# Another fixed order for the prologue of a decoder layer: weight casts ahead of the second half's norm halves, keys evicted first

## The chip, the cores and the metric

The kernel runs on one core of one Trainium2 chip. The metric is the time of one execution on the device in microseconds (us), lower is better; the kernel is run three times and the median stands for it. One of the executions was recorded by the hardware profiler, and all rows shown below are from that one.

A core has five engines with an instruction queue each: PE (TensorE, matrix products; PEld is its weight load), DVE (VectorE), ACT (ScalarE), POOL (GpSimd) and SP (SyncE, which here issues all DMA transfers). [...]

## The reference, cut to what matters

A decoder layer on x of 8 sequences x 128 tokens x 512 features, float32:

```python
x = x + attn(layernorm(x), w_q, w_k, w_v, w_o)   # 32 query heads, 8 key heads, head size 128, causal
x = x + xattn(ctx, ctx, layernorm(x))            # softmax over keys of ctx, no weights
x = x + ffn(layernorm(x), gate, up, down)        # 4-bit weights with scales and zeros, silu(gate)*up
```

Only the start of the first line is touched here: the norm of x, the products with w_q (512 x 4096), w_k and w_v (512 x 1024 each), and the first attention steps. The first line's heart is

```python
q = (h @ w_q).reshape(B, S, 8, 4, 128); k = (h @ w_k).reshape(B, S, 8, 128); v = ...
scores = einsum("bqhgd,bkhd->bhgqk", q, k) * 128 ** -0.5
probs = softmax(where(causal, scores, -inf)); attn = einsum("bhgqk,bkhd->bqhgd", probs, v)
return attn.reshape(B, S, 4096) @ w_o
```

## The kernel before, in words

**Two halves per number.** Products are made of 16-bit pieces: each operand is held as a high float16 part and a low one (the rest), and a product takes three matmuls (`mm3`, L161 to L163: high x high, high x low, low x high). So nearly each tile is made in two steps: ACT casts the high part (`split`, L115), then DVE or POOL subtracts it from the source for the low part (L118). For weights that are cast "direct", ACT scales and casts (`convert`, L349) and DVE makes the low part (L350).

**Weight scales.** A weight tile is scaled by a power of two that is found from its squares: `sumsq` (L259, ACT, squares with a running sum), then `scales_parts`: a copy on DVE (L282), a tiny matmul with ones that adds over partitions (L286 or L289, into ps_n), and three small DVE steps (L295, L303, L311). `next(...)` on such a generator emits its next part.

**Norm.** A tile of x (128 tokens, xr0 to xr7) gets its mean and variance on DVE (`ln_stats`, L400 to L406), then POOL raises the variance to -1/2 (rstd, L412) and writes the normed tile h (L414) in `ln_apply`. The tiles are handled in two halves of four. The first half's h is transposed on TensorE (`h_pe`, L392, then split by ACT and DVE into hT). The second half's h takes another way (`h_dma`): ACT casts the high half hb (L115), POOL makes the low half (L118), and SP issues a DMA transpose into hT (L431).

**Groups and tiles.** The work goes by groups of one key head and its four query heads (8 groups, 2 halves). `proj_k` makes a group's keys for a half (512 tokens), `proj_q` one of its four query heads, `proj_v` the values for one tile of 128 tokens and a pair of groups. Their results land in a PSUM bank each (ps_k, ps_q, ps_v, all of one ring of two banks) and are evicted by ACT and DVE in the generators' second part: keys to k2 (L115, L118), queries to qh and ql, values to v (L494, L495), followed by two DMA copies vd of the value's first rows (L501). `att_s` is an attention step's first part: score matmuls (ps_sc), mask and row maximum (DVE, L558), exponential (ACT, L515), scaling by the sums (POOL, L525 and L572), the split into pb (ACT cast L115, POOL low part L118), and a DMA transpose of pb to pt (L586); pb has two buffers, pt three. `att_v` multiplies pt with the values (ps_at, L595 and on), `att_o` with w_o (ps_o), added to xr (L612).

**What sets the order.** The program is built by a tile scheduler that orders instructions by its own estimate of time. The prologue is kept out of that: everything that `begin()` emits is chained inside `in_order()`, which ties each instruction to the one before it on the same engine. So the order of the calls in `begin()` is the order on each engine, with one exception: instructions whose names are in `loose` are free, and these are those of `att_s(0, 0)`. After `begin()` the scheduler decides, so a change in `begin()` also moves later instructions about; which of them stay where they are can be seen only in the built program. The store zd (L734) puts the unpacked 4-bit zeros, made by DVE (L721) from zw (L715), into memory, from where they are read back spread over the partitions (zi, L750); srow (L637) are the scales of the same weights.

All DMA transfers are issued by SP from one queue. The first 13 (x, and the weights of the first group) are issued at once.

Of the kernel before, what the change touches and what calls it, by code (L numbers as in the profile page):

```python
# [23 lines left out]
GH = 4  # L24
NH = 32
HB = 4
# [27 lines left out]
def tile_decoder(  # L54
# [19 lines left out]
    nc = tc.nc  # L74
# [56 lines left out]
    loose = set()  # L131
# [109 lines left out]
    def sumsq(kind, g, i, j, n=1):  # L241

        raw = raw_t[kind, g]
        if kind == "q":
            view = raw[:, :, j * P : (j + 1) * P]
        elif kind == "c":
            view = raw.unsqueeze(1)
        elif kind in "kv":
            view = raw
        else:  # L250
            view = raw[:, i * GH // n : (i + 1) * GH // n, :]
        key = "ss", kind, g
        if key not in raw_t:
            cols = GH if kind == "q" else n
            raw_t[key] = small.tile([P, cols], F32, name="ss" + kind, tag="ss" + kind)
        col = j if kind == "q" else i
        junk = work.tile([P, 2 * TH], BF16, name="junk", tag="junk", bufs=1)
        free = view.shape[1] * view.shape[2]
        ins = nc.scalar.activation(  # L259
            junk[:, :free].rearrange("p (a t) -> p a t", a=view.shape[1]),  # L260
            view,
            AF.Square,
            accum_out=raw_t[key][:, col : col + 1],
        )
        if pace:
            issue_after(ins, pace["exp"])
        return ins
# [5 lines left out]
    def scales_parts(kind, g, cols=None):  # L273

        ss = raw_t["ss", kind, g]
        n = ss.shape[1]
        c0, c1 = cols or (0, n)
        m = c1 - c0  # L280
        sb = small.tile([P, m], BF16, name="sb", tag=f"sb{m}")
        nc.vector.tensor_copy(sb, ss[:, c0:c1])  # L282
        ps = bank("a", [P, GH], "ps_n")
        w = m if kind == "q" else 1
        if w == m:
            nc.tensor.matmul(ps[:, :w], ones, sb, start=True, stop=True)  # L286
        else:
            for i in range(m):
                nc.tensor.matmul(  # L289
                    ps[:, :1], ones, sb[:, i : i + 1], start=i == 0, stop=i == m - 1  # L290
                )
        yield
        norm = ONORM if kind == "o" else WNORM
        r = small.tile([P, w], F32, name="r", tag=f"r{w}")
        nc.vector.tensor_scalar(  # L295
            r.bitcast(I32),
            ps[:, :w].bitcast(I32),
            0x7F000000,
            1,
            ALU.bitwise_and,  # L300
            ALU.logical_shift_right,
        )
        nc.vector.tensor_scalar(r, r, ROOT, 2.0**64 / norm, ALU.max, ALU.mult)  # L303
        if kind == "c":
            sc_t[kind, g] = scx[:, g : g + 1]
        if (kind, g) not in sc_t:
            sc_t[kind, g] = small.tile(
                [P, GH if kind == "q" else 1], F32, name="sc" + kind, tag="sc" + kind
            )
        sc = sc_t[kind, g]  # L310
        nc.vector.reciprocal(sc[:, c0:c1] if kind == "q" else sc, r)  # L311
        yield
# [50 lines left out]
    def prep_wq(g, j, direct=False):  # L363
        hi = wqp.tile([P, KT, P], F16, name="wqh", tag="wqh")
        lo = wqp.tile([P, KT, P], F16, name="wql", tag="wql")
        wq_t[g * GH + j] = hi, lo
        raw = raw_t["q", g][:, :, j * P : (j + 1) * P]
        return convert(hi, lo, raw, sc_t["q", g][:, j : j + 1], direct)
# [28 lines left out]
    def ln_stats(b):  # L397
        st = small.tile([P, 6], F32, name="st", tag="st")
        mv = small.tile([P, 2], F32, name="mv", tag="mv")
        nc.vector.bn_stats(st, xr[b])  # L400
        nc.vector.bn_aggr(mv, st)
        rs = small.tile([P, 2], F32, name="rs2", tag="rs2")
        nc.vector.tensor_scalar(
            rs[:, 0:1], mv[:, 1:2], EPS, ASCALE**-2, ALU.add, ALU.mult
        )
        nc.vector.tensor_scalar(rs[:, 1:2], mv[:, 0:1], -1.0, None, ALU.mult)  # L406
        ln_t["rs", b] = rs

    def ln_apply(b):
        rs = ln_t.pop(("rs", b))  # L410
        rstd = small.tile([P, 1], F32, name="rstd", tag="rstd")
        nc.gpsimd.tensor_tensor(rstd, rs[:, 0:1], mhalf, ALU.pow)  # L412
        h = deqp.tile([P, H], F32, name="h", tag=("qr", "zi")[b % 2], bufs=2)
        nc.gpsimd.tensor_scalar(h, xr[b], rs[:, 1:2], rstd, ALU.add, ALU.mult)  # L414
        ln_t["h", b] = h
# [30 lines left out]
    def proj_q(g, half, j, pieces=(slice(0, TH),)):  # L446

        ps = bank("j", [P, TH], "ps_q")
        if j % 2 == 0:
            q_t[g, half, j // 2] = [  # L450
                qp.tile([P, HB, 2, 2, HQ], F16, name="q" + p, tag="q" + p) for p in "hl"
            ]
        hi, lo = q_t[g, half, j // 2]
        for cs in pieces:
            proj(ps[:, cs], wq_t[g * GH + j], half, cs)
            yield
            bs = slice(cs.start // P, cs.stop // P)
            split(
                hi[:, bs, :, j % 2, :],
                lo[:, bs, :, j % 2, :],  # L460
                ps[:, cs].rearrange("p (b a t) -> p b a t", a=2, t=HQ),
            )
            yield
# [300 lines left out]
    for m in "gud":  # L764
        _, _, _, ngr, n = quant[m]
# [9 lines left out]
    def begin():  # L775

        warm = const.tile([P, TH], BF16, name="warm")
        nc.vector.memset(warm, 0.0)
        psw = bank("s", [P, TH], "ps_w")

        def fill(n):
            for _ in range(n):
                nc.tensor.matmul(psw, warm[:, :P], warm, start=True, stop=True)

        fill(11)
        load_x(0)
        fetch_wk(0)
        for b in range(1, HB):
            load_x(b)
        fetch_wq(0)  # L790
        fetch_wv(0)
        for b in range(HB, B):
            load_x(b)
        fetch_wo(0)
        fetch_wk(1)

        kgen = proj_k(0, 0, ((0, 2), (2, 4)))
        h = {b: h_pe(b) for b in range(HB)}
        q = [proj_q(0, 0, j) for j in range(GH)]
        ln_stats(0)  # L800
        sumsq("k", 0, 0, 0)
        ln_apply(0)
        sk = scales_parts("k", 0)
        next(sk)
        ln_stats(1)
        next(sk)
        ln_apply(1)
        next(h[0])
        fill(6)
        ln_stats(2)  # L810
        ln_apply(2)
        next(h[0])
        next(h[1])
        fill(5)
        ln_stats(3)
        ln_apply(3)
        prep_wk(0, True)
        next(h[1])
        next(h[2])
        sumsq("q", 0, 0, 0)  # L820
        sq = scales_parts("q", 0, (0, 1))
        next(sq)
        fill(2)
        next(h[2])
        next(sq)
        next(h[3])
        prep_wq(0, 0, True)
        next(kgen)
        next(h[3])
        for j in range(1, GH):  # L830
            sumsq("q", 0, 0, j)
        next(kgen)
        sq, sv, so = scales_parts("q", 0, (1, GH)), scales_parts("v", 0), scales_parts("o", 0)
        next(sq)
        ln_stats(4)
        ln_apply(4)

        next(q[0])
        next(sq)
        prep_wq(0, 1, True)  # L840
        next(kgen)
        sumsq("v", 0, 0, 0)
        next(sv)
        h_dma(4)
        ln_stats(5)
        ln_apply(5)
        next(q[0])
        next(sv)
        next(q[1])
        prep_wq(0, 2, True)  # L850
        h_dma(5)
        ln_stats(6)
        ln_apply(6)
        prep_wq(0, 3, True)
        next(q[1])
        next(q[2])
        h_dma(6)
        ln_stats(7)
        ln_apply(7)
        prep_wv(0, 0, True)  # L860
        soft_scale(0)
        next(q[2])
        next(q[3])
        last_h = h_dma(7)
        fetch_wq(1)
        prep_wv(0, 1, True)
        v = [proj_v(0, b) for b in range(HB)]
        next(q[3])
        next(v[0])
        n = len(nc.cur_bb.bb.instructions)  # L870
        att_s(0, 0)
        loose.update(i.name for i in nc.cur_bb.bb.instructions[n:])
        next(v[1])
        next(v[0])
        next(v[2])
        next(v[1])
        next(v[3])
        next(v[2])
        next(v[3])
        for i in range(2):  # L880
            sumsq("o", 0, i, 0, 2)
        for _ in so:
            pass
        out_scale(0)
        prep_wo(0, 0, True)
        prep_wo(0, 1, True)
        return last_h

    with in_order():
        last_h = begin()  # L890
# [467 lines left out]
```

## Time and profile before

| | us |
|---|---|
| median of 3 runs | 669.97 (669.09 to 671.97) |
| the profiled execution | 669.99 |
| its span, first to last instruction | 668.2 |
| TensorE busy | 632.3 (95%) |
| DVE, ACT, POOL busy | 478.1, 443.3, 389.4 |
| TensorE idle from 12.6 to 35 us | 5.69 |
| TensorE idle from 35 to 55 us | 3.72 |
| TensorE idle from 55 to 90 us | 0.05 |

Times within the profile count from the start of the span. A row of the timeline gives start and duration, engine, line, operation, what is written and read with the shapes, how many are merged, and in brackets the idle time of the engine before it with the instruction that ended it. TensorE ran at its full clock (granted share 0.999), and its weight loads overlap its matmuls.

### The profile page before, as it was taken

Reading aid. Unit: us, or ns where it says so; the run is one execution under the profiler, and the core shown is the slowest. Engines: PE = TensorE matmul, PEld = TensorE weight load, DVE = VectorE, ACT = ScalarE, POOL = GpSimd, SP = SyncE. Lnnn points to the kernel's source line nnn. Section 1 sums busy time; section 2 is a strip of 40 time slices with the busy share of each in tenths; the row PEclk is TensorE's granted clock in tenths of the full one; section 3 lists DMA queues with packets and bytes.
Section 4 is the critical chain, followed back from the end, with each engine's and each line's share of the span. In section 5 each row is a group of like instructions: output and inputs, shape, how many; then the busy total and the mean of one; then the engine's idle time right before and its main releaser. Section 6 shows DMA issues by size and latency. Waiting matters only on the chain.

```text
span 668.2 us, 12402 instructions
## 1 busy us (share of the span) xinstructions
PE 632.3 (95%) x3978; PEld 339.1 (51%) x3978; DVE 478.1 (72%) x1492; ACT 443.3 (66%) x1239; POOL 389.4 (58%) x576
## 2 busy tenths in 40 slices
PE   7798999999999999999999999999998989899996
PEld 4365545455555556555555555445544434444442
DVE  6756687765757776675778465677676779889896
ACT  4587486655757575656678566875566478977774
POOL 5668297744747795556588587753577247422520
PEclk9999999999999999999999999999999999999999
DMA  9266344854454665455445624143543252102002
GB/s 311 51 161 172 100 62 122 170 119 149 111 153 96 180 134 153 102 153 141 146 117 150 147 36 119 46 102 72 87 60 69 39 85 51 34 18 63 2 1 63
DMA packets 117757, 69.34 MB, mean 104 GB/s; under 512 B 84174, under 2 KB 100577, under 8 KB 117692
## 3 DMA queue, kind: packets, MB, share of 16 engines
q1 hardware_dynamic: 117692, 68.55, 43.1%
q8 instruction: 31, 0.51, 0.3%
q14 instruction: 34, 0.28, 0.1%
HBM read 42.12 MB, written 2.20 MB: 66 GB/s over the span
## 4 chain that ended last, share of the span: by engine, by line
PE 49%; POOL 18%; issue 9%; DMA 8%; DVE 8%; ACT 7%; SPq 0%; POOLq 0%; DVEq 0%; ACTq 0%
PE ps_c L1093 6%; PE ps_c L1094 6%; PE ps_o L163 5%; PE ps_o L161 5%; PE ps_o L162 5%; DMA pt<-pb 4%; PE ps_q L161 4%; PE ps_q L163 4%; PE ps_q L162 4%; POOL pb L118 4%; POOL s L572 3%; DMA rawq<-in_L_attn_w_q_dram 2%; POOL wql L118 2%; POOL wol L118 2%; POOL rawo L355 2%
## 5 line engine op out<-in xcount | busy, mean ns | idle before, releaser
L515 ACT ACTIVATE s<-s,negm 128x64 f32<-128x64 f32 (+1 forms) x256 | 93.2, 367 | 35.6 <-DVE negm L558 35.4
L161 PE MATMUL ps_o<-woh,ah 128*128 128x512 f16 x256 | 97.1, 379 | 2.4 <-ACT ah L115 2.2
L161 PE MATMUL ps_q<-hT,wqh 128*128 128x512 f16 x256 | 97.0, 379 | 1.9 <-DVE ql L118 1.0
L163 PE MATMUL ps_o<-woh,al 128*128 128x512 f16 x256 | 97.1, 379 | 1.5 <-DVE al L118 1.4
L162 PE MATMUL ps_o<-wol,ah 128*128 128x512 f16 x256 | 97.0, 379 | 0.0
L163 PE MATMUL ps_q<-hT,wql 128*128 128x512 f16 x256 | 97.0, 379 | 0.0
L162 PE MATMUL ps_q<-hT,wqh 128*128 128x512 f16 x256 | 97.0, 379 | 0.0
L612 DVE SCALAR_TENSOR_TENSOR xr<-ps_o,unsc,xr 128x512 f32<-128x512 f32 x64 | 47.9, 748 | 43.4 <-PE ps_o L163 40.6
L118 POOL TENSOR_TENSOR pb<-s,pb 128x256 f16<-128x256 f32 (+1 forms) x128 | 71.9, 577 | 11.1 <-ACT pb L115 8.4
L558 DVE CUSTOM_DVE_ANT_0 s<-ps_sc,mask,soft 128x64 f32<-128x64 f32 (+1 forms) x256 | 67.2, 311 | 6.5 <-PE ps_sc L163 4.7
L525 POOL TENSOR_SCALAR rec<-rec 128x4 f32<-128x4 f32 x64 | 14.9, 233 | 93.8 <-DVE rec L523 91.9
L572 POOL TENSOR_TENSOR s<-s,rec 128x128 f32<-128x128 f32 (+1 forms) x128 | 63.9, 520 | 4.5
L118 DVE TENSOR_TENSOR ql<-ps_q,qh 128x512 f16<-128x512 f32 x64 | 44.0, 687 | 29.3 <-ACT qh L115 29.1
L115 ACT CAST pb<-s 128x128 f16<-128x128 f32 (+1 forms) x128 | 43.3, 351 | 30.7 <-POOL s L572 29.3
L115 ACT CAST ah<-ps_at 128x512 f16<-128x512 f32 x64 | 37.2, 582 | 19.1 <-PE ps_n L289 7.1
L355 POOL TENSOR_TENSOR rawo<-rawo,sco 128x512 f32<-128x512 f32 x30 | 31.5, 1056 | 29.9 <-DVE sco L311 29.9
L515 ACT ACTIVATION_READ_ACCUMULATOR s<-s,negm 128x1 f32 x256 | 48.5, 190 | 0.0
L118 DVE TENSOR_TENSOR al<-ps_at,ah 128x512 f16<-128x512 f32 x64 | 43.8, 684 | 4.7 <-ACT ah L115 4.2
L115 ACT CAST qh<-ps_q 128x512 f16<-128x512 f32 x64 | 36.8, 575 | 15.3 <-PE ps_q L163 15.2
L1102 ACT ACTIVATE ps_c<-ps_c,rTu 128x512 f32<-128x512 f32 (+1 forms) x57 | 36.7, 662 | 14.7 <-PE ps_c L1094 14.4
L1104 DVE TENSOR_SCALAR ps_c<-ps_c,rTg 128x512 f32<-128x512 f32 (+1 forms) x56 | 40.5, 750 | 7.2 <-PE ps_c L1094 7.1
L161 PE MATMUL ps_sc<-k,qh 128*128 128x128 f16 (+1 forms) x256 | 41.2, 206 | 2.7 <-ACT qh L115 2.6
(225 smaller groups left out, 1737.7 us busy)
## 6 DMA issues: line engine op xcount, KB each, us to landing
rawq<-in_L_attn_w_q_dram SPq DMA_DIRECT2D x8, 1024.0 KB, 7.0
rawo<-in_L_attn_w_o_dram SPq DMA_DIRECT2D x8, 1024.0 KB, 6.0
zi<-zd SPq DMA_DIRECT2D x26, 256.0 KB, 3.6
vd<-v SPq DMA_DIRECT2D x64, 64.0 KB, 2.3
qr<-_L_ffn_down_qweight_dram SPq DMA_DIRECT2D x10, 256.0 KB, 3.5
xr<-in_x_dram SPq DMA_DIRECT2D x8, 256.0 KB, 5.2
rawk<-in_L_attn_w_k_dram SPq DMA_DIRECT2D x8, 256.0 KB, 3.4
rawv<-in_L_attn_w_v_dram SPq DMA_DIRECT2D x4, 512.0 KB, 7.6
```

The costliest lines, as they stand in the source:

```text
L115: a = nc.scalar.copy(hi, src)
L118: b = (lo_eng or nc.vector).tensor_tensor(lo, src, hi, ALU.subtract)
L161: nc.tensor.matmul(ps, lh, rh, start=start and i == 0, stop=False)
L162: nc.tensor.matmul(ps, lh, rl, start=False, stop=False)
L163: nc.tensor.matmul(ps, ll, rh, start=False, stop=stop and i == n - 1)
L355: a = nc.gpsimd.tensor_tensor(raw, raw, wide.to_broadcast(list(raw.shape)), ALU.mult)
L515: exp = nc.scalar.activation(v, v, AF.Exp, bias=negm[:, j : j + 1], scale=-1.0, accum_out=sums[:, j : j + 1],)
L558: nc.vector.tensor_tensor_reduce(view, flat(ps, cols[j]), masks[j // 2], soft_t[g][:, j % 2 : j % 2 + 1], BIG, ALU.add, ALU.min, negm,)
L572: mul = nc.gpsimd.tensor_tensor(v, v, rec[:, 2 * k : 2 * k + 2].unsqueeze(2).to_broadcast([P, 2, (k + 1) * HQ]), ALU.mult,)
L612: return nc.vector.scalar_tensor_tensor(xr[b], ps, unsc_t[g], xr[b], ALU.mult, ALU.add)
L1093: nc.tensor.matmul(ps, lh, rh, start=r == 0, stop=False, skip_group_check=r > 0)
L1104: nc.vector.tensor_scalar(ps, ps, sc, None, ALU.mult)
```

## The change

`begin()` is written in another order; no call is added or taken away. In the new order

- the statistics and the norm of tile 3 (`ln_stats(3)`, `ln_apply(3)`) come ahead of the second part of the transposes of tiles 0 and 1, and those of tile 4 ahead of the cast of the first query weight;
- the squares of the query weights are no longer taken three in a row: that of query 1 comes ahead of tile 4's statistics, those of 2 and 3 behind both halves of the key product, and the eviction of the keys (the third `next(kgen)`) comes ahead of `h_dma(4)` and the second query weight's cast;
- the query weights 1, 2 and 3 are cast (`prep_wq`) ahead of `h_dma(5)`, and both value weights (`prep_wv`) ahead of `h_dma(6)` and `h_dma(7)`; the squares and the scale of the value weight come behind the second and third query weight's cast;
- `h_dma(6)` and `h_dma(7)` stand behind most of the query evictions;
- the matmuls of `att_s(0, 0)` are no longer free: only its instructions on other engines are in `loose`;
- the generators of v and of w_o's scales are made at another place, which emits nothing.

```diff
@@ -797,6 +797,7 @@
         kgen = proj_k(0, 0, ((0, 2), (2, 4)))
         h = {b: h_pe(b) for b in range(HB)}
         q = [proj_q(0, 0, j) for j in range(GH)]
+        v = [proj_v(0, b) for b in range(HB)]
         ln_stats(0)
         sumsq("k", 0, 0, 0)
         ln_apply(0)
@@ -809,67 +810,69 @@
         fill(6)
         ln_stats(2)
         ln_apply(2)
+        ln_stats(3)
+        ln_apply(3)
         next(h[0])
         next(h[1])
         fill(5)
-        ln_stats(3)
-        ln_apply(3)
+        next(h[1])
         prep_wk(0, True)
-        next(h[1])
         next(h[2])
         sumsq("q", 0, 0, 0)
-        sq = scales_parts("q", 0, (0, 1))
-        next(sq)
+        sq0 = scales_parts("q", 0, (0, 1))
+        next(sq0)
+        next(h[2])
+        next(h[3])
         fill(2)
-        next(h[2])
-        next(sq)
+        next(sq0)
         next(h[3])
+        sumsq("q", 0, 0, 1)
+        ln_stats(4)
+        ln_apply(4)
         prep_wq(0, 0, True)
         next(kgen)
-        next(h[3])
-        for j in range(1, GH):
-            sumsq("q", 0, 0, j)
         next(kgen)
-        sq, sv, so = scales_parts("q", 0, (1, GH)), scales_parts("v", 0), scales_parts("o", 0)
+        sumsq("q", 0, 0, 2)
+        sumsq("q", 0, 0, 3)
+        sq = scales_parts("q", 0, (1, GH))
         next(sq)
-        ln_stats(4)
-        ln_apply(4)
-
         next(q[0])
         next(sq)
+        next(kgen)
+        h_dma(4)
         prep_wq(0, 1, True)
-        next(kgen)
-        sumsq("v", 0, 0, 0)
-        next(sv)
-        h_dma(4)
         ln_stats(5)
         ln_apply(5)
+        prep_wq(0, 2, True)
+        sumsq("v", 0, 0, 0)
         next(q[0])
+        next(q[1])
+        prep_wq(0, 3, True)
+        sv = scales_parts("v", 0)
+        next(sv)
+        h_dma(5)
         next(sv)
         next(q[1])
-        prep_wq(0, 2, True)
-        h_dma(5)
+        next(q[2])
         ln_stats(6)
         ln_apply(6)
-        prep_wq(0, 3, True)
-        next(q[1])
+        prep_wv(0, 0, True)
+        prep_wv(0, 1, True)
         next(q[2])
-        h_dma(6)
         ln_stats(7)
         ln_apply(7)
-        prep_wv(0, 0, True)
         soft_scale(0)
-        next(q[2])
+        h_dma(6)
+        next(q[3])
         next(q[3])
         last_h = h_dma(7)
         fetch_wq(1)
-        prep_wv(0, 1, True)
-        v = [proj_v(0, b) for b in range(HB)]
-        next(q[3])
         next(v[0])
         n = len(nc.cur_bb.bb.instructions)
         att_s(0, 0)
-        loose.update(i.name for i in nc.cur_bb.bb.instructions[n:])
+        loose.update(
+            i.name for i in nc.cur_bb.bb.instructions[n:] if i.engine != mybir.EngineType.PE
+        )
         next(v[1])
         next(v[0])
         next(v[2])
@@ -877,6 +880,7 @@
         next(v[3])
         next(v[2])
         next(v[3])
+        so = scales_parts("o", 0)
         for i in range(2):
             sumsq("o", 0, i, 0, 2)
         for _ in so:
```

## The prediction

> **What bounds the kernel now.** I read the page first, then busy time by stretches, then each engine's timeline through the prologue.
>
> ```profile
> PE 632.3 (95%) x3978; PEld 339.1 (51%) x3978; DVE 478.1 (72%) x1492; ACT 443.3 (66%) x1239; POOL 389.4 (58%) x576
> 12.60:35.00 22.40, 16.71 (x108) 9.12 (x107) 14.90 (x41) 12.65 (x25) 11.23 (x12) 1.00 0.43 113
> 35.00:55.00 20.00, 16.28 (x136) 10.90 (x135) 11.44 (x54) 18.01 (x66) 13.12 (x24) 1.00 0.73 188
> 55.00:90.00 35.00, 34.95 (x225) 19.15 (x223) 23.59 (x87) 21.22 (x60) 19.81 (x26) 1.00 0.42 100
> ```
>
> The stretches give length, then busy time of PE, PE's weight loads, DVE, ACT, POOL. TensorE is full from 55 us (34.95 of 35). Before that it idles 22.40 - 16.71 = 5.69 us and 20.00 - 16.28 = 3.72 us. The matmuls are the same in both kernels, so whatever the new order takes out of these 9.41 us should move the rest forward. TensorE's timeline shows where the idle time lies (start, duration, then in brackets the idle time and its releaser):
>
> ```profile
> 20.35 0.16 PE L286 MATMUL ps_n<-sb,ones 128*128 128x1 bf16 x1 [1.30 <-DVE sb L282]
> 26.87 0.38 PE L161 MATMUL ps_q<-hT,wqh 128*128 128x512 f16 x1 [1.01 <-DVE ql L118]
> 31.16 0.27 PE L161 MATMUL ps_v<-wvh,hT 128*128 128x256 f16 x1 [1.48 <-DVE ql L118]
> 33.73 0.27 PE L162 MATMUL ps_v<-wvl,hT 128*128 128x256 f16 x1 [0.40 <-DVE wvl L350]
> 46.26 0.39 PE L161 MATMUL ps_q<-hT,wqh 128*128 128x512 f16 x1 [0.86 <-DVE r L303]
> 52.76 0.20 PE L161 MATMUL ps_sc<-k,qh 128*128 128x64 f16 x1 [2.43 <-ACT qh L115]
> ```
>
> A matmul's row lasts 0.38 us, though the next one starts 0.22 us later, so each printed gap is about 0.16 us below the matmul time lost. With that, and with gaps of 0.81, 0.23, 0.75 and 0.37 us at 14.85, 16.27, 32.56 and 33.04, I count 7.0 us lost up to 35 us and, with 0.59 at 53.48, 4.3 us from there to 55 us.
>
> Why the evictions and weights are late is seen on ACT and POOL:
>
> ```profile
> 23.80 0.62 ACT L115 CAST hb<-h 128x512 f16<-128x512 f32 x1 [2.08 <-POOL h L414]
> 24.33 0.72 ACT L349 ACTIVATE wqh<-rawq,scq 128x512 f16<-128x512 f32 x1
> 24.51 1.16 POOL L118 TENSOR_TENSOR hb<-h,hb 128x512 f16<-128x512 f32 x1 [0.74 <-ACT hb L115]
> 25.62 1.01 POOL L412 TENSOR_TENSOR rstd<-rs,mhalf 128x1 f32<-128x1 f32 x1
> 26.73 0.77 POOL L414 TENSOR_SCALAR h<-xr,rs,rstd 128x512 f32<-128x512 f32 x1
> 27.54 0.62 ACT L115 CAST hb<-h 128x512 f16<-128x512 f32 x1 [2.02 <-POOL h L414]
> 31.27 0.62 ACT L115 CAST hb<-h 128x512 f16<-128x512 f32 x1 [2.02 <-POOL h L414]
> ```
>
> This is a ring with one turn in 3.73 us (27.54 - 23.80; 31.27 - 27.54). ACT waits 2.0 us for POOL's h, three times. Behind that wait, in ACT's order, stand a weight cast and a query eviction that don't need h: wqh for query 3 at 24.33, wvh at 28.06 and 31.80. So the norm of the second half's tiles, wanted only at 40 us, paces the first half's weights, wanted at once.
>
> [...] the weight's scale was ready at 17.8 us and its cast waited until 24.33. [...] the cast's low half (L350) takes 0.75 us at 18.62 but 1.13 us at 25.08, under POOL's 1.16 us at 24.51; then rstd (L412) takes 1.01 us at 25.62 instead of 0.55. [...] vd at 36.31 us, behind the 1 MB rawq of 34.48, took 4.3 us to land, where the vd issued from 43 to 46 us took 2.0.
>
> **The change, part by part.** No instruction is added or removed. I laid the new order end to end, each instruction at the later of its engine being free and its inputs being there, with durations from these rows. All new times below are such estimates. The first 13 loads stay in place.
>
> *Keys evicted and statistics taken earlier.* Statistics of tile 4 (0.68, 0.18 and two of 0.15 us) stand ahead of the first query weight and start at 13.8 instead of 16.1; rstd follows at 15.0 (17.4 before) and h ends at 16.8 (18.8). The key eviction comes before the second query weight's cast and runs at 15.7 (18.5). Cost: the squares of query weights 2 and 3 end later against the small norm matmul, which waits 0.71 us (0.23 before). That is the price of this part, 0.5 us.
>
> *Weight casts ahead of the norm halves.* The scale of weights 1 to 3 is there at 16.9. ACT casts at 17.4, 18.0 and 20.2 (before 17.87, 21.00, 24.33; 0.62 us apart). [...] The V scale comes later, since its squares (1.06 us) stand behind two casts: its copy runs on DVE at 22.8 and its small matmul at 23.0, with TensorE waiting 1.40 us (as before, 1.47). V casts: 23.7 and 24.4 (before 28.06, 31.80); low halves done at 27.0 (33.7).
>
> TensorE then: query 0 16.2 to 18.7, query 1 to 21.6 (0.27 us wait for its low weight), query 2 23.0 to 25.6, query 3 to 28.1, first V to 29.4, then 0.58 us for query 3's low half, and no gap until the first half's last V at 35.8. That was at 40.02. Lost time: 0.71 + 0.27 + 1.40 + 0.58 = 3.0 against 7.0: **4.0 us**.
>
> *Score matmuls held in order.* The first scores no longer slip between query matmuls. They are 12 matmuls of under 0.06 us spacing; moving them costs nothing but the 0.58 us counted, which stalls the next V with them.
>
> *Norm halves behind.* POOL: rstd of tile 5 at 20.4, tile 6 at 25.4, tile 7 at 28.7; the last two low halves (1.16 us each) end at 31.2 and 32.3. Their transposes wait on SP one behind the other (1.24 us to issue), are issued at 31.2 and 32.5, and land 3.1 us later, the last at 35.6 (before: 33.15 and some 36.2). The second half's keys need all four, and TensorE comes there at 35.8. What was 3.8 us of slack is 0.2: this edit is free only just.
>
> *SP queue.* The next rawq goes out at 33.8 instead of 34.48, still behind the four transposes. The zeros and scale loads (zw, srow) now follow the first two attention transposes pt. Before, SP sat in `38.26 3.11 SPq L501` until rawq had landed and issued the first pt at 43.19; pb has two buffers, so ACT's third pb cast waited for that landing (46.04), the fourth until 48.65, and the query eviction behind them came at 52.13: the 2.43 us gap. New: pt at 37.5, landing at 41.6 behind rawq, and the next at about 44; the casts run at 41.6 and 45.1. The gap becomes 1.27 us; those beside it stay (1.2 and 0.6). Saved: **1.2 us**.
>
> Sum: 4.0 + 1.2 = 5.2, of which I take 5.1. From the second half's keys on, the large order on TensorE is the same but for interleavings, and what it waits for there moves along. The profiled run took 669.99 us, 1.8 outside its span of 668.2; the median of the runs is 669.97. Span 663.1, time **664.9 us**.
>
> **Rivals.**
>
> *Given back in part.* The norm of tiles 5 to 7 becomes the bound: slack is 0.2 us, and the weights' low halves now stand close together on DVE, each able to hold POOL 0.46 us (1.01 - 0.55). Two or three more collisions, or transposes 1.24 us apart landing slower than the lone ones seen, put the last landing at 36.8 to 38: TensorE waits 1 to 2.2 us, gain 2.9 to 4.1, time 666 to 667. For it: the thin slack. Against: I have two such holds in the sum already. Chance 0.18.
>
> *More than counted.* Waits of attention for pt after 90 us (0.71 us at 93.81 printed, three others) belong to an interleaving that changes; if they go, 2 to 3 us more, about 662. Nothing in the profile asks for it. Chance 0.07.
>
> *Slower.* The pt ahead of 93.81 stands behind the store zd:
>
> ```profile
> 86.90 0.26 SPq L734 DMA_DIRECT2D zd<-z  x1
> 87.36 2.05 SPq L586 DMA_TRANSPOSE pt<-pb  x1
> 92.96 0.83 SPq L750 DMA_DIRECT2D zi<-zd  x2
> ```
>
> zi waits for zd's landing, so zd takes 6.06 us and holds that pt with it, and TensorE already waits there. zd hangs on zw, which is loaded 7.4 us later now (42.5 for 35.07). Each us by which zd comes after 81.8 (86.90 - 5.1) is lost in full; at 86.9 the gain is gone, and past 90.3 the kernel is slower by over 0.5%; at 91 it takes 674 us. Against: zw lands by 46 and DVE first reads it after 60. Chance 0.04.
>
> That the change does nothing is excluded: the orders differ on all engines.
>
> **How the numbers follow.** 0.5%, 3.35 us, is about what a measurement of this kernel tells from no change. The likeliest case has 0.71, with 663 to 666.5 as its own range. Faster by over 0.5% (below 666.6): 0.71, 0.07 and a third of the 0.18, less a little for the edge of the likeliest: 0.82. Within 0.5%: 0.14. Slower: 0.04. The range, 662.3 to 667.8, leaves out the slower case and the ends of the others.
>
> **What would show it.** Right: ACT's 2.0 us waits before hb (L115) gone as a series, wvh casts near 24, second-half keys on TensorE near 36, idle up to 55 us down from 9.4 to about 4.9 as printed. Wrong: a TensorE wait of over 1 us before the second half's ps_k released by hT's transpose (first rival); a longer wait at ps_at behind zd (third); wql or rstd rows above 1 us in most rounds.

## The result, and the profile after

The changed kernel takes 667.36 us (median of 8 runs, 665.86 to 668.79) against 670.06 us of the kernel before: a ratio of 0.9955, 95% interval 0.9937 to 0.9972. In a second comparison, with runs of the kernel before on the same chip beside it, it took 666.58 us (5 runs, 666.11 to 668.30) against 670.88: 0.9944, interval 0.9930 to 0.9957. It is faster, by 2.7 and 4.3 us where 5.1 were predicted; 667.4 lies within the range of 662.3 to 667.8 and above the likeliest case's own range of 663 to 666.5.

The first profiled execution took 668.19 us (span 666.4), the one of the second comparison 666.48 (span 664.7). I call the two profiles the first and the second one after. The same three stretches as before, columns as there (length; busy time of PE, PE's weight loads, DVE, ACT, POOL; then granted clock, DMA share, GB/s), in the first profile after:

```profile
12.60:35.00 22.40, 20.34 (x155) 12.82 (x155) 18.27 (x66) 15.31 (x41) 12.26 (x14) 1.00 0.47 113
35.00:55.00 20.00, 16.08 (x102) 8.72 (x100) 10.10 (x36) 15.90 (x53) 14.73 (x25) 0.92 0.89 198
55.00:90.00 35.00, 35.00 (x224) 19.24 (x223) 23.21 (x93) 22.09 (x66) 20.03 (x28) 1.00 0.47 100
```

and the second of them in the second profile:

```profile
35.00:55.00 20.00, 15.99 (x103) 8.87 (x101) 9.91 (x36) 15.83 (x52) 14.98 (x25) 1.00 0.90 204
```

Up to 35 us TensorE's idle time fell from 5.69 to 2.06 us. From there to 55 us it rose, from 3.72 to 3.92 and 4.01 us. The gain of the first stretch is kept; the second stretch, where 1.2 us were promised, gave nothing. (The granted clock of 0.92 in the first profile is taken up at the end.)

TensorE's timeline of the first profile after says where (start, duration, and in brackets the idle time and its releaser):

```profile
23.36 0.16 PE L286 MATMUL ps_n<-sb,ones 128*128 128x1 bf16 x1 [0.79 <-DVE sb L282]
31.09 0.20 PE L163 MATMUL ps_sc<-k,ql 128*128 128x64 f16 x1 [0.54 <-DVE ql L118]
...
36.93 0.39 PE L161 MATMUL ps_k<-hT,wkh 128*128 128x512 f16 x1
...
46.80 0.28 PE L161 MATMUL ps_v<-wvh,hT 128*128 128x256 f16 x1 [0.87 <-DVE ql L118]
50.04 0.20 PE L161 MATMUL ps_sc<-k,qh 128*128 128x64 f16 x1 [1.75 <-ACT qh L115]
```

Counted as in the prediction (start of a matmul, minus the start of the one before, minus that one's own pace), the waits from 12.6 to 35 us were 7.0 us before and are 2.9 us now: 0.60 at 16.79, 0.41 at 20.24, 0.95 at 23.36, 0.23 at 28.79, and 0.70 at 31.09. The second half's keys start at 36.93 us, and at 36.59 in the second profile, against 40.02. After that, the wait of 1.00 us at 43.17 stayed as it was, that before the scores fell only from 2.59 to 1.92 us (50.04), and one of 1.03 us at 46.80 is new.

ACT and SP show why. First SP, then ACT, of the first profile after (start, time on the engine; for SP the time to issue):

```profile
35.18 0.54 SPq L219 DMA_DIRECT2D rawq<-in_L_attn_w_q_dram  x1
35.81 3.08 SPq L501 DMA_DIRECT2D vd<-v  x5
38.99 1.34 SPq L586 DMA_TRANSPOSE pt<-pb  x1
```

```profile
44.32 0.61 ACT L115 CAST pb<-s 128x256 f16<-128x256 f32 x2 [1.94 <-DMA pt<-pb]
...
46.55 1.32 ACT L349 ACTIVATE woh<-rawo,sco 128x512 f16<-128x512 f32 x2
47.78 0.59 ACT L115 CAST pb<-s 128x256 f16<-128x256 f32 x2
...
49.41 0.58 ACT L115 CAST qh<-ps_q 128x512 f16<-128x512 f32 x1
```

The first pt goes out at 38.99 and lands at 44.25 (by its semaphore in the trace). Until then ACT waits 1.94 us in front of its third pb cast. The square of rawq that stands behind that cast starts only at 44.83, though rawq had landed at 41.32: here ACT took nothing out of turn. From 44.32 to 49.41, for 5.09 us, it works without a pause through two pairs of pb casts, three squares, a query eviction and three woh casts, and only then makes the qh for which TensorE stands still.

### The profile page after: what moved, and what is told of

It reads as the page before. It is cut to its first block, busy times and chain, and to the rows that moved or that the text cites. A ratio compares the mean times of both kernels' runs of the same rounds, so it can differ in the third digit from the quotient of the medians.

```text
span 666.4 us, 12404 instructions
## 1 busy us (share of the span) xinstructions
PE 633.2 (95%) x3978; PEld 339.7 (51%) x3978; DVE 474.1 (71%) x1492; ACT 444.4 (67%) x1239; POOL 389.3 (58%) x576
## 4 chain that ended last, share of the span: by engine, by line
PE 49%; POOL 19%; issue 10%; DVE 8%; DMA 7%; ACT 6%; SPq 0%; POOLq 0%; DVEq 0%; ACTq 0%
PE ps_c L1097 6%; PE ps_c L1098 6%; PE ps_o L163 5%; PE ps_o L161 4%; PE ps_o L162 4%; POOL pb L118 4%; PE ps_q L161 4%; PE ps_q L163 4%; PE ps_q L162 4%; DMA pt<-pb 4%; POOL s L572 4%; POOL wql L118 2%; POOL wol L118 2%; POOL rawo L355 2%; POOL rawq L355 2%
## 5 line engine op out<-in xcount | busy, mean ns | idle before, releaser
L115 ACT CAST pb<-s 128x256 f16<-128x256 f32 (+1 forms) x128 | 43.4, 352 | 30.4 <-POOL s L572 27.8
L163 PE MATMUL ps_sc<-k,ql 128*128 128x128 f16 (+1 forms) x256 | 42.7, 206 | 1.1 <-DVE ql L118 1.0
```

The source lines that it names most:

```text
L115: a = nc.scalar.copy(hi, src)
L163: nc.tensor.matmul(ps, ll, rh, start=False, stop=stop and i == n - 1)
```

## The experiments

Two theories stood after this. A: rawq, the 1 MB load that is issued ahead of pt, holds pt back, and with it pb and qh. D, which came up after the first four runs: what stands ahead of qh in ACT's own order holds it back, whenever pt lands. They do not exclude each other: qh comes after both. Waits are given as counted above, and each ratio is to runs of the kernel before beside it on the same chip (medians of 670.85 us for e1 to e4, 670.88 for e7 to e9, 670.60 for e10 and e11).

| kernel | median us | ratio to before, 95% interval |
|---|---|---|
| change, first / second comparison | 667.36 / 666.58 | 0.9955 [0.9937, 0.9972] / 0.9944 [0.9930, 0.9957] |
| e1, change with rawq early | 667.65 | 0.9951 [0.9934, 0.9968] |
| e2, change with the scores loose | 668.86 | 0.9963 [0.9947, 0.9979] |
| e3, first part alone | 670.42 | 0.9992 [0.9982, 1.0001] |
| e4, second part alone | 669.47 | 0.9981 [0.9971, 0.9991] |
| e7, change with woh behind qh | 664.70 | 0.9908 [0.9894, 0.9921] |
| e8, as e7, rawq early | 663.67 | 0.9892 [0.9878, 0.9905] |
| e9, as e8, two squares behind qh too | 660.99 | 0.9851 [0.9838, 0.9864] |
| e10, as e9, rawq back | 662.70 | 0.9881 [0.9859, 0.9903] |
| e11, before, woh and squares behind qh | 666.62 | 0.9942 [0.9925, 0.9960] |

### The two parts alone (e3, e4)

e3 is the kernel before with the change's lines up to the key eviction; from there it is as before:

```diff
         ln_apply(2)
+        ln_stats(3)
+        ln_apply(3)
         next(h[0])
...
+        sumsq("q", 0, 0, 1)
+        ln_stats(4)
+        ln_apply(4)
         prep_wq(0, 0, True)
...
         next(sq)
+        next(kgen)
         prep_wq(0, 1, True)
-        next(kgen)
         sumsq("v", 0, 0, 0)
         next(sv)
```

> The kernel before with the first part of the change alone: keys evicted first, statistics of tiles 3 and 4 sooner, squares of the query weights spread; the weight casts stay behind the norm halves as before. If the gain comes from the casts' place (the prediction), ACT's waits of about 2.0 us before hb stay, and the time is within 0.7 us of the kernel before (669.3 to 670.7). If the early statistics carry the gain, 667 to 668.

e4 is the reverse: the old order up to the first query projection, the change's order from the key eviction on.

> The kernel before with the second part of the change alone: weight casts ahead of the norm halves of tiles 5 to 7, scores' matmuls in order, the scale loads behind the attention transposes; keys and early statistics as before. If the casts' place carries the gain, ACT's waits of 2.0 us before hb go and the time is 2 to 3 us below the kernel before (667 to 668), about the changed kernel's. If the early statistics are needed for it, it stays within 1 us of the kernel before, with TensorE waiting for the first query weights near 20 us or for tile 4 to 7's transposes near 36 us.

e3 measured 670.42 us against 670.85, with the interval just reaching 1: little or nothing, as expected from it. In its profile ACT waits in the old ring:

```profile
23.23 0.62 ACT L115 CAST hb<-h 128x512 f16<-128x512 f32 x1 [2.08 <-POOL h L414]
23.75 0.72 ACT L349 ACTIVATE wqh<-rawq,scq 128x512 f16<-128x512 f32 x1
```

e4 measured 669.47 us, 1.4 below before, between the two outcomes that I had named (2 to 3, or less than 1). The second half's keys start at 38.35 us, so it gets about half of the 3.1 to 3.4 us by which the change moves them. What it lacks shows on TensorE:

```profile
20.46 0.39 PE L161 MATMUL ps_q<-hT,wqh 128*128 128x512 f16 x1 [1.07 <-ACT wqh L349]
```

and on ACT, where an hb cast waits ahead of those weights:

```profile
19.16 0.62 ACT L115 CAST hb<-h 128x512 f16<-128x512 f32 x1 [1.99 <-POOL h L414]
19.69 1.33 ACT L349 ACTIVATE wqh<-rawq,scq 128x512 f16<-128x512 f32 x2
```

In the changed kernel that hb cast, of tile 4, waits 0.77 us and starts at 17.77, since tile 4's statistics were taken earlier. So the parts seem not to be additive: alone they give 0.4 and 1.4 us, together 2.7 to 4.3. With such differences the times alone leave this likely, not sure; TensorE's waits are the better sign. The prediction treated the first part as a price of 0.5 us for the second. It is rather what lets the casts start: without it TensorE waits 1.24 us at 20.46 and 0.72 us at 21.62 for the query weights, against 0.41 us with it.

### The scores loose again (e2)

```diff
-        loose.update(
-            i.name for i in nc.cur_bb.bb.instructions[n:] if i.engine != mybir.EngineType.PE
-        )
+        loose.update(i.name for i in nc.cur_bb.bb.instructions[n:])
```

> The changed kernel with one part undone: the matmuls of the first scores may slip between those of the query and V projections again, as in the kernel before. By the prediction this part costs nothing but moves a wait of 0.5 us: time within 0.5 us of the changed kernel. Rival: held in order, the scores make the following V matmuls wait for query 3's low half (0.70 us of lost time at 31.09), and loose they give 0.5 to 0.7 us back.

668.86 us, with runs from 666.16 to 670.06: unclear against the changed kernel. The first score matmuls do move ahead of query 3, but the wait for ql stays (0.88 us at 30.84, 0.70 in the change), so the rival, that holding them costs 0.5 to 0.7 us, finds no support: the wait was not given back. The second half's keys then wait 0.84 us for the last hT transpose (37.37). The scheduler also ordered many later instructions differently here, so I read no more into the time.

### rawq out of pt's way (e1), and the measure (a2)

```diff
         h_dma(5)
+        fetch_wq(1)
         next(sv)
...
         last_h = h_dma(7)
-        fetch_wq(1)
         next(v[0])
```

> The changed kernel with one edit: the 1 MB load of the next query weights (rawq) is issued right behind the transpose of tile 5's norm halves instead of behind that of tile 7, so some 9 us earlier on SP. Theory A (the second term of the prediction failed because the first attention transpose pt stood behind rawq): the first pt lands by 42 us instead of 44.25, ACT's wait of 1.94 us before its third pb cast shrinks below 0.5, TensorE's new gap of 1.03 us at 46.80 goes and the one of 1.92 at 50.04 falls to about 1; the time is 1.0 to 1.5 us below the changed kernel, about 665.5 to 666. Theory B (the five vd transfers hold pt, rawq doesn't matter): pt lands within 0.5 us of where it did, time within 0.5 us of the changed kernel. Theory C (rawq only moves its harm): the transposes of tiles 6 and 7 land 1 to 2 us later than at 35.98 and 36.88, TensorE waits for them before the second half's keys, and the time is that of the changed kernel or 1 us above it.

> The changed kernel, unaltered, as the measure for the three beside it and as a second look at TensorE's clock. If the half-clock stretch at 51 to 56 us and the fixed gaps of 1.03 us at 46.80 and 1.92 us at 50.04 belong to the order, the gaps come back within 0.2 us, while the stretch comes back only in some executions; the time is 667 to 668 at a mean clock of 0.995 to 0.999.

TensorE's order is the same as in the changed kernel. ACT's is not: the scheduler put the second pb cast (45.36) ahead of a square and two woh casts (46.49), which stand ahead of it in the changed kernel (46.55, then the cast at 47.78). SP and ACT in e1's profile:

```profile
27.34 0.54 SPq L219 DMA_DIRECT2D rawq<-in_L_attn_w_q_dram  x1
...
39.88 1.24 SPq L586 DMA_TRANSPOSE pt<-pb  x1
```

```profile
42.71 0.60 ACT L115 CAST pb<-s 128x256 f16<-128x256 f32 x2
...
45.36 0.60 ACT L115 CAST pb<-s 128x128 f16<-128x128 f32 x2 [0.95 <-DMA pt<-pb]
46.49 1.32 ACT L349 ACTIVATE woh<-rawo,sco 128x512 f16<-128x512 f32 x2
...
48.84 0.57 ACT L115 CAST qh<-ps_q 128x512 f16<-128x512 f32 x1
```

pt now lands 2.75 us after its issue (39.88 to 42.63), not 5.26; the vd ahead of it take 2.2 to 3.2 us, not 5.6 to 6.5; the transposes of tiles 6 and 7 land as before (3.51 and 3.14 us; 3.52 and 3.09 in the change). So rawq was what held pt; theories B and C fail. ACT's wait of 1.94 us and TensorE's of 1.03 us are gone, and the scores start 12.15 us after the second half's keys instead of 13.11: the stretch is 1.0 us shorter. But the wait before the scores is 2.01 us, where theory A had about 1, and the time is not to be told from the changed kernel's.

The length of that wait misleads here. It stayed because TensorE comes to it 1.0 us sooner as well. And ACT's new order costs qh something: ACT stands 0.95 us for the second pt (which lands at 45.28) with a square and two woh casts ready behind, and from 45.36 works without a pause up to qh. In the changed kernel's order it would need 5.09 us from the cast at 42.71, so that qh would come at 47.80 instead of 48.84 and the wait would be about 1.0 us, as theory A had it. This is an estimate from the rows of both profiles; no run has rawq early with ACT's order kept. So e1 neither bears out nor refutes that part of theory A. It did show how much ready work stands ahead of qh, and theory D was formed here.

The unaltered change on the next chip (a2) showed the same waits: 1.01 us at 46.45 and 1.91 us at 49.67.

### The work ahead of qh (e7, e8, e9)

e7 takes the four woh casts out of the prologue and ties them behind the second query eviction of the second half:

```diff
-        prep_wo(0, 0, True)
-        prep_wo(0, 1, True)
...
-    for j in range(2, GH):
-        prep_wo(0, j)
...
+        if i == 0:
+            for j in (0, 1, 2, 3):
+                cast = prep_wo(0, j, j < 2)[j // 2]
+                issue_after(cast, q_ev[0, 1, 1][0])
```

where q_ev keeps the instructions that evict a query head. e8 adds e1's edit. e9 adds

```diff
-    for j in range(GH):
+    for j in range(2):
         sumsq("q", 1, 0, j)
...
+            for j in (2, 3):
+                issue_after(sumsq("q", 1, 0, j), q_ev[0, 1, 1][0])
```

with the scales that hang on these squares moved behind them.

> The changed kernel, with the four casts of the first output weights (woh, about 0.6 us of ACT each) held behind the second eviction of the second half's queries (qh) on ACT. Theory D: TensorE's gap of 1.92 us at 50.04 is not the attention transposes' any more but work that stands ahead of qh in ACT's order (three woh casts and four squares of rawq, with no idle time from 44.3 to 49.4 us); then qh comes about 1.2 us sooner, the gap falls below 1.0 us, and the time is 0.5 to 1.2 us below the changed kernel. Theory A (pt and pb alone set it): the gap stays within 0.3 us. A cost is possible: if the woh casts come too late for the first output matmuls (near 60 us), a new wait of up to 1 us stands there.

> Both edits: rawq's load early, woh casts behind qh. Theory D: the gaps of 46.80 and 50.04 both shrink, together by 2.0 us or more against the changed kernel, and the time is 1.0 to 2.0 us below it. If either of the two waits returns elsewhere before 60 us, less than 0.7 us.

> As the run before, and the last two squares of rawq (0.72 us of ACT each) held behind qh as well; the first attention's second part moves ahead on TensorE with it. Theory D: the gap before the second half's scores vanishes (below 0.3 us), 0.5 to 1.0 us more than the run before. Rival: the next group's query weights, which hang on those squares, come late, and TensorE waits for wqh or for the first pt for 1 us or more before 70 us.

Against the changed kernel on the same chip (666.58): e7 is 1.9 us faster, e8 2.9, e9 5.6, each more than expected. In e7 the second qh starts at 48.38, 11.18 us after the keys instead of 12.48, and TensorE no longer waits for it. What it waits for now, 0.83 us just ahead of the scores, is a small norm matmul that needs the sums (sb) of rawq's squares:

```profile
48.91 0.16 PE L286 MATMUL ps_n<-sb,ones 128*128 128x4 bf16 x1 [0.67 <-DVE sb L282]
```

So theory D holds: the place of the woh casts costs TensorE time while pt is as late as before, and theory A alone fails. In e8, with rawq early as well, the wait at 46.80 is gone (0.71 us in e7), and 0.77 us are left before the small matmul and 0.24 before the scores. The runs of e8 (663.14 to 663.89) all lie below those of e7 (664.17 to 665.05): rawq's place is worth 1.0 us here, as much as e1's profile showed between keys and scores.

Not all of the gain lies in the prologue. The waits from 36 to 60 us are 5.0 us in the second profile after, 3.9 in e7 and 3.3 in e8. The changed kernel also waits 1.18 us at 123.91 and 0.86 us at 151.93 for a pt, and in e7 and e8 both waits are gone. The scheduler orders these stretches itself; why the waits went was not examined. In e9 ACT reaches qh at 46.30:

```profile
45.16 0.60 ACT L115 CAST pb<-s 128x128 f16<-128x128 f32 x2 [0.48 <-DMA pt<-pb]
...
46.30 0.56 ACT L115 CAST qh<-ps_q 128x512 f16<-128x512 f32 x1
```

and TensorE is full in the stretch that was emptiest:

```profile
35.00:55.00 20.00, 19.76 (x134) 11.51 (x132) 10.38 (x38) 16.60 (x55) 12.96 (x23) 1.00 0.66 151
```

e9 gains more than I expected for it (2.7 us over e8, not 0.5 to 1.0). With it the scheduler also puts the first attention's products (ps_at, and one of ps_o) ahead of or among the second half's scores on TensorE, which fill the time in which qh is made and part of the old wait of 1.00 us at 43.17 (0.35 at 43.36), and the wait for pt near 90 us went (0.98 us in a2, 1.15 in e8, 0.18 in e9); a new one of 0.83 us stands at 146.20. From 36 to 60 us e9 waits 0.8 us, e8 3.3. These effects of one edit were not taken apart. The expected rival, late weights of the next group, did not come: no wait of over 0.2 us stands between 44 and 100 us.

### The same without rawq's move, and on the kernel before (e10, e11)

e10 is e9 with rawq back in its place; e11 is the kernel before with the edits of e9 to woh and squares alone.

> The fastest edit so far (woh casts and the last two squares of rawq held behind qh), with rawq's load back where the changed kernel has it, ahead of the first attention transpose. If rawq in front of pt costs what the earlier pair of runs gave (1.0 us), or more because less is left on ACT to hide it, this run is 1 to 2 us slower than the one with rawq early (about 662 to 663), and TensorE waits again between 44 and 48 us. If qh's place alone carried the gain, it stays within 0.4 us of 661.

> The kernel before, its prologue's order untouched, with the same casts and squares held behind qh. In that order ACT also works through three woh casts and squares without idle time ahead of qh (48.65 to 52.13 us), and TensorE waits 2.59 us there. Theory D: that wait goes below 1 us and the time is 1.5 to 3.5 us below the kernel before (667.4 to 669.4), so the edit is independent of the change under study and adds to it. If it needs the new order, within 0.7 us of the kernel before.

e10 took 662.70 us (660.48 to 664.77), as expected 1 to 2 us above e9, though on another chip. The wait has moved to the matmul that needs pt itself:

```profile
44.23 0.27 PE L597 MATMUL ps_at<-pt,vd 128*128 128x256 f16 x1 [1.65 <-DMA pt<-pb]
```

e11 took 666.62 us against 670.60, 4.0 us less, a little more than expected. On TensorE the wait of 1.00 us at 46.26 is gone, one of 0.48 for pt stands there, and the 2.59 us before the scores are 0.44. A new wait of 0.50 us, for woh at 51.77, is the price of casting it later:

```profile
51.15 0.20 PE L161 MATMUL ps_sc<-k,qh 128*128 128x64 f16 x1 [0.28 <-ACT qh L115]
```

From 36 to 60 us e11 waits 1.4 us instead of 4.3; another 1.25 us is a wait for pt at 127.13 in the kernel before that e11 no longer has. So an edit of two other places, without the change under study, gives as much as the change, and the two together give about their sum: e9 lies 9.9 us below the kernel before, the change 4.3 of that on the same chip, e11 4.0 on another, rawq's place some 1 to 1.7. e9 is the fastest kernel of this study, 1.5% below the one before (ratio 0.9851).

## Why the prediction was right and wrong

**Weight casts ahead of the norm halves (4.0 us): right in mechanism, 3.6 to 3.7 in size.** From TensorE's second transposes (the ps_x that need tile 1's h) to the first key matmul of the second half it takes 31.56 us in the profile before and 31.38 in e11, which has the same prologue; it takes 27.84 and 27.77 in the two profiles after, and 27.78 to 27.94 in five more kernels with the change's order (e1, e7 to e10). That is 3.6 to 3.7 us, and it takes both parts of the change: e3 has 31.78 us there and e4 29.39. The start in the profile before was itself early by chance: those transposes began at 8.46 us there, at 9.17 in e11, at 9.09 and 8.82 after. So from the profiles as they stand only 3.1 and 3.4 us are seen (40.02 to 36.93 and 36.59), where I had the keys "near 36".

The single waits came out as 0.60, 0.41, 0.95 and 0.70 for 0.71, 0.27, 1.40 and 0.58, with 0.23 not foreseen. The wvh casts came at 24.83, not at 23.7, behind an hb cast that waits:

```profile
23.83 0.62 ACT L115 CAST hb<-h 128x512 f16<-128x512 f32 x1 [2.06 <-POOL h L414]
...
24.83 1.34 ACT L349 ACTIVATE wvh<-rawv,scv 128x512 f16<-128x512 f32 x2
...
28.81 0.62 ACT L115 CAST hb<-h 128x512 f16<-128x512 f32 x1 [2.05 <-POOL h L414]
```

This also shows a sign that I named wrongly. ACT's waits of 2.0 us did not go "as a series": they are still there, 2.06, 2.05 and 1.44 us. What changed is what stands behind them. All the first half's weights but wvh are cast ahead of the wait at 23.83, and nothing that TensorE needs at once stands behind the other two except evictions. A wait that the edit leaves in place but empties of followers is as good as gone, and the number to watch was TensorE's, not ACT's. One sign of being wrong came up as well, without harm: rstd took over 1 us in three of its four rounds (1.06, 1.05, 1.07 and 0.55). Each of the three long ones started 0.1 us after a low half of a weight (L350) on DVE (15.81 after 15.71, 21.34 after 21.24, 26.81 after 26.72), the short one, at 29.90, beside none.

**Norm halves behind: right.** The last two transposes land at 35.98 and 36.88 us, TensorE starts the keys at 36.93 after a wait of 0.15 (0.18 in the second profile). The slack of 0.2 us was used up without harm; e2, with a wait of 0.84 us there, shows how thin it was. The first rival (given back in part, at this place) is therefore not what took the missing time.

**Scores in order: right** as far as e2 can say; the wait that goes with it was 0.70 for 0.58 us.

**SP queue (1.2 us): wrong, by the landing of the first pt.** pt was to be issued at 37.5 and to land at 41.6 "behind rawq", 5.8 us after the second half's keys (35.8). It was issued at 38.99, behind five vd, and landed at 44.25, 7.3 us after the keys (36.93). The prediction names only rawq ahead of it (which landed at 41.32), not the five vd (landing at 41.95 to 43.96) that stand between the two. Here the landings kept the order of the issues (rawq at 35.18, the five vd from 35.81 to 38.35, pt at 38.99); in e1, with rawq early, pt took 2.75 us to land, not 5.26. (The 4.3 us that the prediction gives for "vd at 36.31" are the median of the three vd issued from 36 to 38.5 us.)

These 1.5 us come back on TensorE. 1.03 us are the new wait at 46.80, for the ql of a query whose qh (45.46) stands on ACT behind the late pb cast. 0.65 us are the wait before the scores, 1.92 us where 1.27 were forecast; the wait at 43.17 is 0.2 us shorter than forecast. In place of 1.2 us gained, the stretch from the second half's keys to the first output matmul took 21.28 us before and 21.77 in the second profile after: 0.5 us lost.

ACT's own work ahead of qh is not what failed. The prediction laid this work out in ACT's order and reckoned with it: it has the pb casts at 41.6 and 45.1, 3.5 us apart, though its second pt lands at about 44; the trace has 3.46 us (44.32 to 47.78). Its wait of 1.27 us puts qh some 5.1 us behind the first of these casts (an estimate: before, TensorE takes 10.15 us from the keys to these scores without the wait, and the scores follow qh by 0.63); the trace has 5.09. This work was counted and taken as given. e7 to e9 and e11 show that it need not be: the kernel before has 3.0 us of squares and woh casts straight ahead of that qh too (49.16 to 52.13, without a wait), and moving them was worth about as much as the whole change.

**The sum.** 3.7 for 4.0, and -0.5 for 1.2, make 3.2 us instead of 5.2; the medians say 2.7 and 4.3. TensorE's idle time up to 55 us is 5.98 us in the first profile after, where about 4.9 was named as the sign of being right. Faster by over 0.5%, which had a chance of 0.82, holds for the second comparison (ratio 0.9944) and not for the first (0.9955). That the time lies in the range is in part luck: one of two terms was lost whole, and the room for it had been left for another reason, the first rival, whose 666 to 667 us come close but whose place, the transposes of the norm halves, lost nothing. The rival "more than counted" failed: the wait for pt after 90 us stayed (0.87 us at 93.81 before, 0.99 at 92.56 after). "Slower" had next to no part: the wait that zd was to lengthen is this one, 0.1 us longer. (The pt behind zd took 6.4 us to land in the profile before; the median of all pt there is 2.8.)

## What to carry to other kernels

To see what an engine's wait costs, look at what stands behind it in that engine's order, not at its length: ACT's three waits for h stayed, and 3.6 us were gained by moving other casts ahead of them. For a transfer behind a large one, count those in between as well: rawq landed at 41.32, five vd of 64 KB up to 43.96, and only then pt, at 44.25. When a matmul waits for an eviction, two things make up the delay: what releases the evicting engine (here pt), and what that engine then has ready ahead of the eviction (here 5.09 us of work). Either can be shortened: rawq's place gave 1.0 us, the woh casts and squares more.

Read an edit's effect in every engine's order. e1 left TensorE's order alone and changed ACT's, and with it the wait that it was to test. And measure a stretch from one fixed matmul to another rather than the length of one wait: in e1 the wait stayed at 2.0 us although the scores came 1.0 us sooner after the keys.

## What the runs showed of the hardware that was not expected

TensorE fell to half its clock (granted share 0.50 from 51.89 to 55.30 us) in the first profile after, and not in the second, of the same program. Two rows of it from TensorE's timeline (start, duration):

```profile
53.22 0.63 PE L163 MATMUL ps_q<-hT,wql 128*128 128x512 f16 x1
53.65 0.63 PE L161 MATMUL ps_q<-hT,wqh 128*128 128x512 f16 x1
```

The matmuls follow each other every 0.43 us instead of 0.215, and last 0.63 us instead of 0.38, from 51.85 to 55.33; the granted clock from 35 to 55 us is 0.92, against 1.00 in the second profile. It cost about 1.4 us: the waits counted from 36 to 56 us were 6.35 us in this profile and 4.95 in the second. e1's profile has such a stretch near 51 to 55 us (0.50 in the two whole slices of 1 us from 52 to 54), e3's one at 32 to 36 us (0.50 from 33 to 35), the others none up to 100 us. What brings it on is not shown. In the first profile no single wait was longer than 1.92 us, and 3.55 us of waits stood close together in the 5.0 us before (1.03, 1.92 and 0.60, from 45.77 to 50.77); the second profile has waits of 1.01 and 1.91 us at nearly the same places, at a granted clock of 1.00. The times go with it: of the 49 runs of the kernel before in the first set of experiments, the seven with a mean clock of 0.991 or 0.992 took 672.6 us on average, the seven with 0.998 or 0.999 took 670.7.
